# Row sums of one adjacency on ScalarE, x loads on GpSimd's queue, and the transposed adjacency stored in quarters

## The chip, the cores and the metric

The kernel runs on one core of a Trainium2 chip. The metric is device time of one execution in microseconds; the time before is the median of three runs. Each engine (TensorE or PE, VectorE or DVE, ScalarE or ACT, GpSimd or POOL, SyncE or SP) takes its instructions in order. Transfers are issued from the queue of an engine, here those of SP, ACT and POOL.

## The reference

Sixteen graphs of N = 1,024 nodes with C = 128 features, each with a dense 0/1 adjacency of 1,024 x 1,024. Layer 0 is a gated graph network of four steps behind a layer norm, layer 1 four graph convolutions with a batch norm over all nodes of all graphs; both add their result to x.

```python
def _gru_cell(m, h, w_ih, w_hh, b_ih, b_hh):
    xr, xz, xn = jnp.split(m @ w_ih.T + b_ih, 3, axis=-1)
    hr, hz, hn = jnp.split(h @ w_hh.T + b_hh, 3, axis=-1)
    r = jax.nn.sigmoid(xr + hr)
    z = jax.nn.sigmoid(xz + hz)
    n = jnp.tanh(xn + r * hn)
    return (1.0 - z) * n + z * h

# layer 0
h = jnp.maximum(_layernorm(x), 0.0)
for i in range(4):
    hw = jnp.einsum('bnc,cd->bnd', h, weight[i])
    m = jnp.einsum('bjn,bjd->bnd', adj, hw)       # adj transposed
    h = _gru_cell(m, h, w_ih[i], w_hh[i], b_ih[i], b_hh[i])
x = x + h * nodemask
# layer 1
h = jnp.maximum(_layernorm(x), 0.0)
for i in range(4):
    h = relu(jnp.einsum('bnm,bmc->bnc', adj, h @ W[i]) + b[i])
    mu, var = mean and variance of h over (batch, node)
    h = gamma[i] * (h - mu) * rsqrt(var + eps) + beta[i]
x = x + h
```

Layer 0 aggregates with the transposed adjacency, layer 1 with the adjacency itself; so one of the two has to be turned.

## The kernel before, in words

Features stay transposed, 128 channels on partitions and nodes in two halves of 512. The kernel has two stages.

**Stage 1 (layer 0)** runs two streams of batches, `sa` (even) and `sb` (odd), against each other. `half_step(one, two)` aggregates for one stream (`agg_step`, line 524: 32 matmuls of 128x512, the features split into a high and a low part) while the gates of the other are computed (line 1000: 24 matmuls). TensorE alternates between these two kinds; ScalarE copies the aggregate `m` (L961) and does the gates' functions (L1018, L1023, L1027), VectorE their products and the low part of the next split (L932, L1019 to L1044). There are 64 such half steps, eight to a pair of batches. The order on all five engines is written by hand here (`tc.manual_schedule`): what the Python code issues first stands first. Side work is put in through an agenda: `at(n, place, go)` names a half step and a place in it, and `due(place)` issues it there ("beside0", "beside1", "gap", "mid" and others are places in `half_step`).

Side work of stage 1 that matters here:

- *Node features.* `next_load` loads the 512 KB of x of the batch after next (L539, 14 loads) on ACT's queue. `norm_sums` (L664, L665) takes their statistics on VectorE within the same or the next half step. `xmid_d` and `ymid_d` (L752, L755) keep what stage 2 needs, stored on POOL's queue.
- *Raw adjacency.* Rows arrive in tiles `stage` on SP's queue and are cast to `row` on GpSimd (L577); `glance` (L586) takes a sum over each on ScalarE.
- *State exchange.* `cross_h` goes out and eight `n_h` come back on SP's queue (L591, L598); the split of the next step needs `n_h`.
- *The transposed adjacency for stage 2.* `transposes` is a generator that one call of `feed.some(n)` moves on by n rows. For a row it casts to bf16 on GpSimd (L615, tile `half`, two buffers) and issues a DMA transpose on SP's queue (L616) into `adjT`, a tile for one batch, of which there is one buffer. After eight rows the whole tile of 2 MB is stored to `adjT_d` from POOL's queue (L629). `Feed` keeps a flag `full` at the eighth row; then nothing more is fed until `mids` has issued the store in that or a later half step, and `next_step` clears the flag. `mids` first issues a small copy `pace` on GpSimd (L1101) that waits for the new state. Rows are fed in three places of a half step, with `counts` of (2, 1, 1), and more in two of a cycle's half steps.

**Stage 2 (layer 1)** loops over 4 layers and 16 batches. `load_adjT` reads a batch's packed adjacency on SP's queue, and casts on VectorE and ScalarE make `wide` from it (L1326, L1328). In layer 0 each batch also has its features split (`first_split`, L1383 to L1386, a ScalarE cast and a VectorE subtraction) and its weights applied to the aggregate (`first_weights`, the copies `cm` at L1395 and the matmuls `pw` at L1396). For the later layers, the batch norm is folded into the weights. The first batch after each batch norm (`raw_split`, `raw_weights`) has to add a term with the sum of every adjacency row; that sum, the same on every partition, lies in `degree` (L1413), which uses the memory of `w_mT` once stage 1 is over. `row_sums` makes it after the aggregation of stage 2's first batch: 16 matmuls of 128x512 with a matrix of ones (L1422) and two copies on ScalarE (L1426).

At the change of stages the order on VectorE and ScalarE is settled by a scheduler; in the last gate steps of stage 1 the order of TensorE, GpSimd and SP is still by hand.

Of the kernel before, what the change touches and what calls it, by code (L numbers as in the profile page):

```python
# [8 lines left out]
F32 = mybir.dt.float32  # L9
F32R = mybir.dt.float32r  # L10
BF16 = mybir.dt.bfloat16
# [5 lines left out]
P = 128  # L17
HALF = 512
# [323 lines left out]
def exact_path(  # L342
# [39 lines left out]
    def tmp(name):  # L382
        return ps_t.tile([P, HALF], F32, tag="tmp", name=name)

    adjT_d = [dram.tile([NB, P, N], BF16, tag=f"adjT{b}", name=f"adjT_d{b}") for b in range(B)]
    xmid_d = [dram.tile([N, C], F32, tag=f"xmid{b}", name=f"xmid_d{b}") for b in range(B)]
    ymid_d = [dram.tile([P, N], F32, tag=f"ymid{b}", name=f"ymid_d{b}") for b in range(B)]
# [10 lines left out]
    def turned_tile(name):  # L398
        return keep.tile([P, NB, N], BF16, tag="adjT", name=name, bufs=1)
# [8 lines left out]
    nc.vector.memset(eps_t, EPS)  # L408
    ones = const.tile([P, 1], F32, tag="ones", name="ones")
    nc.vector.memset(ones, 1.0)  # L410
    low = const.tile([P, (B + 2) * NB], F32, tag="low", name="low")
    nc.vector.memset(low, 0.0)

# [119 lines left out]
    with ExitStack() as st:  # L533
# [3 lines left out]
        def load_x(b, eng):  # L537
            xt = flat(f"x{b}")
            eng.dma_start(xt, x[b].rearrange("(k p) c -> p k c", p=P))  # L539
            return xt  # L540
# [39 lines left out]
        def glance(b, stage, js):  # L580

            junk = work.tile([P, N], BF16, tag="junk", name=f"junk{b}_{js[0]}", bufs=1)
            for j in js:
                lows = stage[j % 4].bitcast(U16).rearrange("p (n t) -> p n t", t=2)[:, :, 0]
                k = b * NB + j
                nc.scalar.activation(junk, lows, AF.Copy, accum_out=low[:, k : k + 1])  # L586

        def exchange_out(t, name, d=None):
            if d is None:
                d = rawd.tile([P, HALF], F32, tag="cross", name=f"cross_{name}", bufs=8)  # L590
            nc.sync.dma_start(d, t)  # L591
            return d
# [19 lines left out]
        def transpose_rows(b, row, j, adjT):  # L612

            t = work.tile([P, N], BF16, tag="half1", name=f"half{b}_{j}", bufs=2)
            nc.gpsimd.tensor_copy(t, row.bitcast(F32))  # L615
            return lambda: nc.sync.dma_start_transpose(adjT[:, :, j * P : (j + 1) * P], t)  # L616

        def transposes(batches):

            for b, rows in batches:  # L620
                adjT = turned_tile(f"adjT{b}")
                ahead = transpose_rows(b, rows[0], 0, adjT)
                for j in range(NB):
                    go = ahead
                    if j + 1 < NB:
                        ahead = transpose_rows(b, rows[j + 1], j + 1, adjT)
                    go()
                    yield j
                nc.gpsimd.dma_start(adjT_d[b].rearrange("k p n -> p k n"), adjT)  # L629
                yield NB  # L630

        class Feed:


            jobs, full, stored = iter(()), False, False

            def some(self, n):
                for _ in range(n):
                    if not self.full:
                        self.full = next(self.jobs, None) == NB - 1  # L640

            def store(self):
                if self.full and not self.stored:
                    self.stored = next(self.jobs) == NB

            def next_step(self):
                if self.stored:
                    self.full = self.stored = False

        feed, agenda = Feed(), {}  # L650

# [118 lines left out]
        class Stream:  # L770
# [35 lines left out]
                norm_blocks(self.xt, self.y, self.norm, ks)  # L806

            def next_load(self):
                self.next_x = load_x(self.b + 2, nc.scalar)

            def next_sums(self):
                self.next_norm = norm_stats(self.next_x, f"in{self.b + 2}")
# [256 lines left out]
        def at(n, place, go):  # L1069
            agenda.setdefault((n, place), []).append(go)  # L1070
# [4 lines left out]

        def first_step(one, two, gated, halfway):

            feed.next_step()
            if one is sa:
                feed.jobs = transposes([(s.b, s.rows) for s in (sa, sb)])  # L1080
            one.split_step()
            feed.some(2)
            two.gate_step(0)
            two.half_away(0)
            if feed.full or (clock[0], "mid") in agenda:
                mids(two)
            feed.some(1)
            two.gate_step(1)
            two.half_away(1)
            gated()  # L1090
            one.agg_step(0)
            halfway()
            feed.some(NB if one is sa else 1)
            one.agg_step(1)
            two.finish()
            clock[0] += 1

        def mids(two):

            pace = small.tile([P, 1], F32, tag="pace", name=f"pace{clock[0]}")  # L1100
            nc.gpsimd.tensor_copy(pace, two.new[:, :1])  # L1101
            feed.store()
            due("mid")

        def half_step(one, two, gated=None, halfway=None):

            feed.next_step()
            counts = (2, 1, 1)
            if one is sb and one.i == 0:
                feed.jobs = transposes([(s.b, s.rows) for s in (sa, sb)])  # L1110
                counts = (0, 0, 0)
            elif two is sb and two.i == 0:
                counts = (2, 2, 1)
            elif two is sa and two.i == 1 and two.across:
                counts = (3, 1, 1)
            due("ins")
            due("start")
            if one.i > 0:
                one.halves_back()
            else:  # L1120
                one.hw = hw_tiles(one.b, f"ghw{one.b}_0")
            two.fetch()
            feed.some(counts[0])
            two.products(0)
            two.reset_gate(0)
            due("beside0")
            due("looks")
            two.fetch_more()
            two.candidate(0)
            two.less(0)  # L1130
            two.update_gate(0)
            two.scaled()
            one.high(0)
            one.low(0)
            two.mixed(0)
            two.half_away(0)
            two.first_four()
            if feed.full or (clock[0], "mid") in agenda:
                mids(two)
            feed.some(counts[1])  # L1140
            two.products(1)
            two.reset_gate(1)
            one.high(1)
            due("beside1")
            two.first_glances()
            one.low(1)
            two.candidate(1)
            two.less(1)
            two.update_gate(1)
            two.last_four()  # L1150
            two.scaled()
            two.mixed(1)
            two.half_away(1)
            due("outs")
            if gated:
                gated()
            due("gap")
            due("end")
            one.agg_step(0)
            if halfway:  # L1160
                halfway()
            feed.some(counts[2])
            one.agg_step(1)
            two.finish()
            clock[0] += 1
# [4 lines left out]
        with tc.manual_schedule(engines=every):  # L1170
# [111 lines left out]
            def ahead(i):  # L1282
                join_layer(i)
                if i + 1 < L:
                    turn_hh(i + 1)

            sa.plan(0)
            sb.plan(1)
            first_step(sa, sb, looks, lambda: ahead(1))
            first_step(sb, sa, lambda: turn_ih(prep, w_g, 2), lambda: ahead(2))  # L1290
            written[0] = False
# [89 lines left out]
    def first_split(b):  # L1381
        yt = flat(f"y{b}").rearrange("p k c -> p (k c)")
        nc.gpsimd.dma_start(yt, ymid_d[b])  # L1383
        hw = hw_tiles(b, f"chw{b}_0")
        nc.scalar.copy(hw[0], yt)
        nc.vector.tensor_sub(hw[1], yt, hw[0].bitcast(F32))  # L1386
        return hw

# [17 lines left out]
    def raw_weights(i, pm, aff, stats):  # L1406
# [6 lines left out]
            nc.vector.scalar_tensor_tensor(mt[:, cols], degree[:, cols], aff[1], mt[:, cols], ALU.mult, ALU.add)  # L1413
            nc.tensor.matmul(pc[hf], w_c[:, i, :], mt[:, cols], start=True, stop=True)
        conv_done(0, i, pc, stats)

    def row_sums(rows):

        pd = [tmp(f"pt_deg{hf}") for hf in range(NH)]
        for j in range(NB):  # L1420
            for hf in range(NH):
                nc.tensor.matmul(  # L1422
                    pd[hf], ones_r, rows[j][:, hf * HALF : (hf + 1) * HALF], start=(j == 0), stop=(j == NB - 1)
                )
        for hf in range(NH):
            nc.scalar.copy(degree[:, hf * HALF : (hf + 1) * HALF], pd[hf])  # L1426

    xo = []

# [29 lines left out]
            for n0, n in pieces(k):  # L1459
                nc.gpsimd.dma_start(xo_piece(k, n0, n), by_node(xmid_d[k], n0, n))  # L1460

    ones_r = work.tile([P, P], F32R, tag="ones_r", name="ones_r", bufs=1)
    nc.vector.tensor_copy(ones_r, ones.to_broadcast([P, P]))
    degree = w_mT.rearrange("p l c -> p (l c)")[:, :N]

    stats = small.tile([P, B * NH, 6], F32, tag="bn_st", name="stats0")
# [1 line left out]
    for b in range(B):  # L1468
        rows = load_adjT(b, 0)
        hw_next = first_split(b + 1) if b + 1 < B else None  # L1470
        pm = banks(b, 0)
        aggregate(pm, hw, rows, 0)
        if waiting:
            last = first_weights(*waiting, stats)
            if b == 1:
                with tc.issue_after(last.ins):
                    sb.rest()
        if b == B - 1:
            hw_next = raw_split(1)
        aggregate(pm, hw, rows, 1)  # L1480
        if b == 0:
            row_sums(rows)
        hw, waiting = hw_next, (b, pm)


# [112 lines left out]
```

## Time and profile before

| | us |
|---|---|
| three runs | 1769.65, 1770.71, 1772.32 |
| median | 1770.71 |
| the profiled execution, time | 1769.17 |
| the profiled execution, span of the core | 1767.4 |
| TensorE busy | 1752.3 |
| VectorE busy | 1289.3 |
| ScalarE busy | 1112.0 |
| GpSimd busy | 362.9 |

The profile is one execution on the chip. The span goes from its first to its last recorded event; 1.8 us of the profiled execution's own time lie around it. A group names its line, engine, operation, and output and input tiles. Busy time of TensorE is close to time that its matmuls follow one another; their durations overlap, so that spacing is read from starts. In a list of waits, three numbers are the total in us, how often, and the longest. A timeline row has start and duration in us, and in brackets the idle time before it with what ended it.

### The profile page before, as it was taken

Reading aid. Unit: us, or ns where it says so; the run is one execution under the profiler, and the core shown is the slowest. Engines: PE = TensorE matmul, PEld = TensorE weight load, DVE = VectorE, ACT = ScalarE, POOL = GpSimd, SP = SyncE. Lnnn points to the kernel's source line nnn. Section 1 sums busy time; section 2 is a strip of 40 time slices with the busy share of each in tenths; the row PEclk is TensorE's granted clock in tenths of the full one; section 3 lists DMA queues with packets and bytes.
Section 4 is the critical chain, followed back from the end, with each engine's and each line's share of the span. In section 5 each row is a group of like instructions: output and inputs, shape, how many; then the busy total and the mean of one; then the engine's idle time right before and its main releaser. Section 6 shows DMA issues by size and latency. Waiting matters only on the chain. (4 is left out here: it accounts for less than half of the span.)

```text
span 1767.4 us, 22310 instructions
## 1 busy us (share of the span) xinstructions
PE 1752.3 (99%) x6734; PEld 1192.7 (67%) x6734; DVE 1289.3 (73%) x2310; ACT 1112.0 (63%) x1713; POOL 362.9 (21%) x401
## 2 busy tenths in 40 slices
PE   9999999999999999999999999999999999999997
PEld 5565656565656565656565656577778888888886
DVE  7677877877877887877887786766666666666665
ACT  5356556557556556655655664487677767767765
POOL 4214213322332331321422323110100000000011
PEclk9999999999999999999999999999999999999999
DMA  7458568577686676776866857887866665757667
GB/s 261 138 169 280 166 180 301 158 223 248 196 214 221 221 212 216 238 197 200 270 185 178 305 137 228 287 290 289 292 220 215 234 243 210 256 202 258 230 220 270
DMA packets 376160, 400.14 MB, mean 226 GB/s; under 512 B 158188, under 2 KB 254224, under 8 KB 376032
## 3 DMA queue, kind: packets, MB, share of 16 engines
q1 hardware_dynamic: 342736, 323.59, 58.0%
q0 software_dynamic: 18208, 67.46, 10.2%
q10 hardware_dynamic: 15088, 7.60, 1.5%
q8 instruction: 54, 0.88, 0.2%
q14 instruction: 74, 0.61, 0.1%
HBM read 267.47 MB, written 97.52 MB: 207 GB/s over the span
## 5 line engine op out<-in xcount | busy, mean ns | idle before, releaser
L524 PE MATMUL pm<-row,ghw 128*128 128x512 f32 x2048 | 503.9, 403 | 0.5 <-POOL row L563 0.3
L524 PEld LDWEIGHTS pm<-row,ghw 128*128 128x128 f32 x2048 | 383.6, 188 | 107.1 <-issue 25.6
L524 PE MATMUL pc_m<-wide,chw 128*128 128x512 f32 x1024 | 245.2, 395 | 0.0
L615 POOL CAST half<-row 128x1024 bf16<-128x1024 f32 x128 | 143.7, 1133 | 402.3 <-DMA adjT<-half 387.4
L524 PEld LDWEIGHTS pc_m<-wide,chw 128*128 128x128 f32 x1024 | 190.4, 188 | 41.9 <-issue 3.8
L961 ACT COPY m<-pm 128x512 f32<-128x512 f32 x128 | 68.7, 588 | 195.4 <-PE pm L524 195.4
L1023 ACT ACTIVATE r<-r,vecs 128x512 f32<-128x512 f32 x128 | 92.2, 721 | 152.8 <-DVE r L1020 148.8
L524 PE MATMUL pc_g_r<-wide,chw 128*128 128x512 f32 x464 | 186.9, 403 | 0.3 <-ACT chw L501 0.3
L1019 DVE SCALAR_TENSOR_TENSOR r<-g_hn,vecs,r 128x512 f32<-128x512 f32 x128 | 93.3, 729 | 128.5 <-ACT r L1018 76.3
L524 PE MATMUL pc_g_z<-wide,chw 128*128 128x512 f32 x464 | 181.0, 390 | 0.0
L577 POOL CAST row<-stage 128x1024 fp32r<-128x1024 f32 x112 | 128.1, 1151 | 207.4 <-DMA stage<-in_adj_dram 198.7
L1328 DVE CAST wide<-block 128x1024 fp32r<-128x1024 bf16 x160 | 110.0, 692 | 73.7 <-PE pc_m L524 36.6
L1328 DVE CAST wide<-packed 128x1024 fp32r<-128x1024 bf16 x160 | 110.1, 691 | 71.8 <-PE pc_g_z L524 53.7
L1326 ACT CAST wide<-packed 128x1024 fp32r<-128x1024 bf16 x96 | 100.7, 1049 | 58.5 <-PE pc_m L524 30.3
L1326 ACT CAST wide<-block 128x1024 fp32r<-128x1024 bf16 x96 | 100.6, 1049 | 53.8 <-PE pc_g_z L524 27.7
L1000 PE MATMUL g_r<-m,w_mT 128*128 128x512 f32 x256 | 130.8, 592 | 0.3 <-ACT m L961 0.3
L1000 PE MATMUL g_z<-m,w_mT 128*128 128x512 f32 x256 | 130.7, 592 | 0.0
L1000 PE MATMUL g_xn<-m,w_mT 128*128 128x512 f32 x256 | 130.7, 592 | 0.0
L1018 ACT ACTIVATE r<-g_r,brz 128x512 f32<-128x512 f32 x128 | 87.9, 686 | 53.9 <-PE g_r L1000 53.4
L1376 DVE BATCH_NORM_STATS2 stats<-feat 128x6 f32<-128x512 f32 x128 | 84.1, 686 | 47.0 <-ACT feat L1375 45.9
L1036 DVE TENSOR_TENSOR h<-h,r 128x512 f32<-128x512 f32 x96 | 78.9, 821 | 54.1 <-ACT r L1023 53.9
L1040 DVE TENSOR_TENSOR h<-h,z 128x512 f32<-128x512 f32 x128 | 105.3, 822 | 14.1 <-ACT z L1027 2.1
(185 smaller groups left out, 2810.8 us busy)
## 6 DMA issues: line engine op xcount, KB each, us to landing
block<-adjT_d SPq DMA_DIRECT2D x256, 256.0 KB, 4.7
packed<-adjT_d SPq DMA_DIRECT2D x256, 256.0 KB, 5.7
stage<-in_adj_dram SPq DMA_DIRECT2D x120, 512.0 KB, 5.4
adjT_d<-adjT POOLq DMA_DIRECT2D x16, 2048.0 KB, 7.8
cross_h<-t_h SPq DMA_DIRECT2D x92, 256.0 KB, 2.1
n_h<-cross_h SPq DMA_DIRECT2D x368, 64.0 KB, 2.0
xmid_d<-x POOLq DMA_DIRECT2D x16, 512.0 KB, 6.7
y<-ymid_d POOLq DMA_DIRECT2D x16, 512.0 KB, 5.2
```

Of the source, the lines that this page charges most:

```text
L524: nc.tensor.matmul(pm[hf], hw[s][:, j * P : (j + 1) * P], rows[j][:, hf * HALF : (hf + 1) * HALF], start=(j == 0 and s == 0), stop=(j == N ...
L577: nc.gpsimd.tensor_copy(t, stage[j % 4])
L615: nc.gpsimd.tensor_copy(t, row.bitcast(F32))
L1000: nc.tensor.matmul(po, wT[:, i, g * C : (g + 1) * C], rhs, start=start, stop=stop)
L1018: nc.scalar.activation(r, pr, AF.Sigmoid, bias=brz[:, 3 * i : 3 * i + 1])
L1019: nc.vector.scalar_tensor_tensor(r, phn, b_hn(i), r, ALU.add, ALU.mult)
L1023: nc.scalar.activation(self.r, self.r, AF.Tanh, bias=b_in(self.i))
L1036: nc.vector.tensor_sub(ho, hin, self.r)
L1040: nc.vector.tensor_mul(ho, ho, self.z)
L1326: nc.scalar.copy(r, t)
L1328: nc.vector.tensor_copy(r, t)
L1376: nc.vector.bn_stats(stats[:, b * NH + hf, :], dst)
```

## The change

It has four parts.

1. The row sums are no longer made by matmuls in stage 2. In stage 1, eight ScalarE instructions (`row_sums` inside `exact_path`'s stage 1, with `accum_out`) sum the rows of batch 0 as they lie in memory: one at each of four places, one in half step 5 and three in half step 6, three in the gap of half step 7, and one at the start of half step 8. At half step 9 POOL's queue stores the 4 KB of sums; at the third batch of stage 2 it loads them back to all partitions, into `degree`. The matrix `ones_r`, the 16 matmuls and the two copies are gone.
2. `next_load` issues on POOL's queue instead of ACT's.
3. `transposes` handles both batches of a pair in one tile, without a stop between them. After every second row, two rows' columns of `adjT` are stored: four stores of 512 KB per batch. The flags of `Feed`, `store` and `next_step` are gone, `counts` is (2, 1, 1) throughout, and `mids` runs only where the agenda has something for "mid".
4. In `first_split` the ScalarE cast is put behind `sb.last_m`, the last copy of an aggregate in stage 1.

```diff
-            for b, rows in batches:
-                adjT = turned_tile(f"adjT{b}")
-                ahead = transpose_rows(b, rows[0], 0, adjT)
-                for j in range(NB):
-                    go = ahead
-                    if j + 1 < NB:
-                        ahead = transpose_rows(b, rows[j + 1], j + 1, adjT)
-                    go()
-                    yield j
-                nc.gpsimd.dma_start(adjT_d[b].rearrange("k p n -> p k n"), adjT)
-                yield NB
+            adjT = turned_tile(f"adjT{batches[0][0]}")
+            steps = [(b, rows, j) for b, rows in batches for j in range(NB)]
+            def cast(s):
+                b, rows, j = steps[s]
+                return transpose_rows(b, rows[j], j, adjT)
+            def store(b, q):
+                cols = slice(2 * q * P, 2 * (q + 1) * P)
+                nc.gpsimd.dma_start(adjT_d[b][:, :, cols].rearrange("k p n -> p k n"), adjT[:, :, cols])
+            ahead = cast(0)
+            for s, (b, rows, j) in enumerate(steps):
+                go = ahead
+                if s + 1 < len(steps):
+                    ahead = cast(s + 1)
+                if s > 1 and s % 2 == 0:
+                    store(steps[s - 1][0], steps[s - 1][2] // 2)
+                go()
+                yield
+            store(steps[-1][0], NB // 2 - 1)
+            yield
...
+        def row_sums(rows, js):
+            for j in js:
+                junk = work.tile([P, N], BF16, tag="junk", name=f"summed{j}", bufs=1)
+                nc.scalar.activation(junk, rows[j].bitcast(F32), AF.Copy, accum_out=by_row[:, j : j + 1])
...
-                self.next_x = load_x(self.b + 2, nc.scalar)
+                self.next_x = load_x(self.b + 2, nc.gpsimd)
...
-            feed.store()
             due("mid")
...
-            feed.next_step()
             counts = (2, 1, 1)
             if one is sb and one.i == 0:
                 feed.jobs = transposes([(s.b, s.rows) for s in (sa, sb)])
                 counts = (0, 0, 0)
-            elif two is sb and two.i == 0:
-                counts = (2, 2, 1)
-            elif two is sa and two.i == 1 and two.across:
-                counts = (3, 1, 1)
...
-            if feed.full or (clock[0], "mid") in agenda:
+            if (clock[0], "mid") in agenda:
                 mids(two)
...
+            for n, place, js in (
+                (5, "beside1", (0,)),
+                (6, "beside0", (1,)),
+                (6, "beside1", (2,)),
+                (6, "gap", (3,)),
+                (7, "gap", (4, 5, 6)),
+                (8, "start", (7,)),
+            ):
+                at(n, place, lambda js=js: row_sums(sa.rows, js))
+            at(9, "mid", lambda: nc.gpsimd.dma_start(degree_d.rearrange("(j p) -> p j", p=P), by_row))
...
-        nc.scalar.copy(hw[0], yt)
+        with tc.issue_after(sb.last_m.ins):
+            nc.scalar.copy(hw[0], yt)
...
-        if b == 0:
-            row_sums(rows)
+        if b == 2:
+            nc.gpsimd.dma_start(degree, degree_d.partition_broadcast(P))
```

More of the change, by code (lines that the diff above doesn't have):

```diff
@@ L383, in tmp @@
         return ps_t.tile([P, HALF], F32, tag="tmp", name=name)
+    degree_d = dram.tile([N], F32, tag="degree", name="degree_d")
     adjT_d = [dram.tile([NB, P, N], BF16, tag=f"adjT{b}", name=f"adjT_d{b}") for b in range(B)]
@@ L410, in exact_path @@
     nc.vector.memset(ones, 1.0)
+    by_row = const.tile([P, NB], F32, tag="by_row", name="by_row")
     low = const.tile([P, (B + 2) * NB], F32, tag="low", name="low")
@@ L618, in transposes @@
         def transposes(batches):
-            for b, rows in batches:
-                adjT = turned_tile(f"adjT{b}")
-                ahead = transpose_rows(b, rows[0], 0, adjT)
-                for j in range(NB):
-                    go = ahead
-                    if j + 1 < NB:
-                        ahead = transpose_rows(b, rows[j + 1], j + 1, adjT)
-                    go()
-                    yield j
-                nc.gpsimd.dma_start(adjT_d[b].rearrange("k p n -> p k n"), adjT)
-                yield NB
+            adjT = turned_tile(f"adjT{batches[0][0]}")
[17 more added lines that the diff above has]
+            yield
         class Feed:
-            jobs, full, stored = iter(()), False, False
+            jobs = iter(())
             def some(self, n):
                 for _ in range(n):
[L639 to L648, printed above, removed]
+                    next(self.jobs, None)
         feed, agenda = Feed(), {}
@@ L1081, in first_step @@
             one.split_step()
-            feed.some(2)
+            feed.some(2 if one is sa else 0)
             two.gate_step(0)
             two.half_away(0)
-            if feed.full or (clock[0], "mid") in agenda:
+            if (clock[0], "mid") in agenda:
                 mids(two)
-            feed.some(1)
+            feed.some(1 if one is sa else 0)
             two.gate_step(1)
@@ L1092, in first_step @@
             halfway()
-            feed.some(NB if one is sa else 1)
+            feed.some(NB - 3 if one is sa else 0)
             one.agg_step(1)
@@ L1101, in mids @@
             nc.gpsimd.tensor_copy(pace, two.new[:, :1])
-            feed.store()
             due("mid")
         def half_step(one, two, gated=None, halfway=None):
-            feed.next_step()
             counts = (2, 1, 1)
@@ L1137, in half_step @@
             two.first_four()
-            if feed.full or (clock[0], "mid") in agenda:
+            if (clock[0], "mid") in agenda:
                 mids(two)
@@ L1415, in raw_weights @@
         conv_done(0, i, pc, stats)
[L1417 to L1426, printed above, removed]
     xo = []
@@ L1460, in fetch_x @@
                 nc.gpsimd.dma_start(xo_piece(k, n0, n), by_node(xmid_d[k], n0, n))
-    ones_r = work.tile([P, P], F32R, tag="ones_r", name="ones_r", bufs=1)
-    nc.vector.tensor_copy(ones_r, ones.to_broadcast([P, P]))
     degree = w_mT.rearrange("p l c -> p (l c)")[:, :N]
```

## The prediction

> **What bounds the kernel now.** I read the page's first two sections, then the waits, then the timelines of the three places that the change touches.
>
> ```profile
> PE 1752.3 (99%) x6734; PEld 1192.7 (67%) x6734; DVE 1289.3 (73%) x2310; ACT 1112.0 (63%) x1713; POOL 362.9 (21%) x401
> PEclk9999999999999999999999999999999999999999
> POOL half L615 <- DMA adjT<-half: 387.4, 66, 18.3
> ACT m L961 <- PE pm L524: 195.4, 62, 5.8
> POOL adjT_d L629 <- DMA adjT<-half: 16.9, 7, 5.1
> ACT ghw L925 <- DMA n_h<-cross_h: 12.4, 13, 2.4
> ```
>
> TensorE is busy 99% of 1767.4 us at full clock. So the time is the number of matmuls times their spacing, plus what TensorE waits, and that is some 15 us in all, most of it at the two ends and in the batchnorm turns, which the change leaves alone. An edit gains only by taking matmuls from TensorE or by ending one of its few waits; it loses by making a new one. Of the waits shown, the 387 us of GpSimd for the transposes cost nothing now (TensorE never waits for them), but they say that GpSimd's queue stands still a good fifth of the time: whatever is put into it in order stands still too. 195 us over 62 waits is ScalarE arriving about 3.15 us early at each half step's `m`: that is its spare time there.
>
> The one stretch in which matmuls go away:
>
> ```profile
> 1158.37 0.39 PE L524 MATMUL pc_g_r<-wide,chw 128*128 128x512 f32 x1
> 1158.77 3.89 PE L1422 MATMUL pt_deg<-wide,ones_r 128*128 128x512 f32 x16
> 1162.50 0.39 PE L524 MATMUL pc_g_z<-wide,chw 128*128 128x512 f32 x1
> ```
>
> Columns: start, duration, work. Starts, not durations, give the cost, since matmuls overlap: L524's are 0.227 us apart (1162.50, 1162.72, 1162.95 ...). From 1158.37 to 1162.50 are 4.13 us; without the 16 they would be 0.23.
>
> The one wait in the middle of the kernel that the change addresses (TensorE, then ScalarE):
>
> ```profile
> 1119.09 1.12 PE L1000 MATMUL g_r<-m,w_mT 128*128 128x512 f32 x2 [0.30 <-ACT m L961]
> 1117.51 1.05 ACT L1385 CAST chw<-y 128x1024 fp32r<-128x1024 f32 x1 [5.77 <-PE pm L524]
> 1118.46 1.07 ACT L961 COPY m<-pm 128x512 f32<-128x512 f32 x2
> ```
>
> The cast for stage 2's first batch got in ahead of the last `m`; the gates wait for `m`.
>
> **The change part by part.**
> *Row sums off TensorE (gain).* 4.13 - 0.23 = 3.90 us, if what follows can come 3.9 us sooner. What is added: 8 ScalarE sums over 128x1024 with an accumulator. The row of that shape is L586, 1.05 us + 0.19 to read the accumulator, spaced about 1.17: 9.4 us on ScalarE in half steps 5 to 8. One at a time they are shorter than the 1.65 us that y blocks (L680) take in the same slots of other half steps without a TensorE wait. The three in half step 7's gap (3.5 us) fit between the end of the square root at 128.85 and `m` at 133.16 with 0.8 to spare. The one at the start of half step 8 delays r by 1.15 us; the low half of the weights is then ready at about 141.95 by the chain, needed 143.4. Cost 0; the cover is ScalarE's spare time, 3.15 us in each of four half steps against 9.4 us of sums, so only a badly placed sum can show: up to 1 us. The two `pt_deg` copies (1.06 us of ScalarE) go. The sums are written once by GpSimd's queue (1,024 runs, as many as xmid_d's: 0.90 to issue, 6.7 to land; in runs of 4 bytes it may be slower, but nothing needs it for 900 us) and read back as 512 KB spread over partitions at the third batch of stage 2; the raw batch's `degree` is wanted only after the layer's statistics, 120 us later. Cost 0, between 0 and 1 us: a gain is excluded, since TensorE waits for nothing there.
>
> *The weight cast put behind the last `m` (gain).* 0.46 + 0.10 us of gaps around 1118.2 to 1119.1 go: 0.56. The cast itself is wanted only at the first aggregation of stage 2, 20 us later. What is late next: nothing until the last gates.
>
> *x from GpSimd's queue (14 loads).* ScalarE is rid of 14 issues of 0.41 us in half steps in which it has 3 us to spare: 0. On GpSimd's queue:
>
> ```profile
> 506.53 0.42 ACTq L539 DMA_DIRECT2D x<-in_x_dram  x1
> 512.37 1.04 POOL L615 CAST half<-row 128x1024 bf16<-128x1024 f32 x1 [11.23 <-DMA adjT<-half]
> 518.43 0.25 DVE L664 BATCH_NORM_STATS2 st_in<-x 128x6 f32<-128x128 f32 x1
> 522.65 0.75 DVE L1019 SCALAR_TENSOR_TENSOR r<-g_hn,vecs,r 128x512 f32<-128x512 f32 x1 [1.00 <-PE g_hn L1000]
> x<-in_x_dram ACTq DMA_DIRECT2D x14, 512.0 KB, 4.6
> xmid_d<-x POOLq DMA_DIRECT2D x16, 512.0 KB, 6.7
> ```
>
> In the changed order x stands right behind that cast, which waits for transposes. So it is issued at about 513.4 + 0.9 of GpSimd's time (xmid_d's row) instead of 506.5, and lands 4.6 to 6.7 us after 513.4: 518.0 to 520.1. VectorE's sums, due at 518.43, start up to 1.7 us late; VectorE idles 1.0 behind them, and its low-part subtraction (L932, ends 527.17) has 2.5 us before the aggregation that begins at 529.71. Late by 1.7, covered by 3.5: cost 0; the other loads, one half step on, have 2.65 us of idle VectorE behind the sums and are 0 to 2 late. Here the Trainium skill speaks against the change: "SBUF — State Buffer", section "SBUF: two separate sides", says that transfers issued by GpSimd have their descriptors written by its cores, which are locked out while VectorE runs a two-port operation, and to issue from ScalarE or SyncE instead. The rows: 512 KB took 4.6 us from ScalarE, 6.7 and 5.2 (y) from GpSimd. By the rule the landing is at the upper end or past it, 2 us late in seven cycles; by the row it is inside the 3.5 us. I take the row: 0. Both ends kept: 0 to +14 (rival 2).
>
> *Four stores of 512 KB in place of one of 2 MB, both batches in one tile.* Per batch GpSimd issues 4 x 0.90 = 3.6 us in place of 0.90 (all rows of GpSimd with about 1,000 runs: adjT_d 0.90, xmid_d 0.90); 16 batches: 43 us more on an engine that is 21% busy and stands waiting for transposes anyhow. The transposes themselves stay 128, at four per half step; a transpose now waits for a quarter's store instead of a whole tile's. A store waits for the landing of its two transposes (2.8 us), and the casts, the x load and the pace copies queue behind it; the next cast needs that transpose's buffer anyway. SyncE: the order of transposes against cross_h and n_h changes; one of 1.25 us now stands between the last cross_h and its eight n_h. In the half steps in question n_h now lands late because the 2 MB store fills the engines (a ghw wait of up to 2.4 us, above, and about 0.55 us left before TensorE would see it). Cutting the store in four takes that away and the transpose puts 1.3 back: even. The skill speaks against small pieces: "DMA: Bandwidth & Descriptors", section "Anatomy of one DMA — SWDGE (gpsimd) path", prices a transfer at 2.0 us + bytes/436e3, so an estimate of 6.8 us for 2 MB (the row: 7.8) and 4 x 3.2 = 12.8 for four. The rows for 512 KB from GpSimd are 3.5 to 6.7. Either way the pieces go out over two half steps (35 us), so the sum by rule and by row is the same 0 for TensorE as long as nobody waits for a store; the last one at the change of stages does matter: reads of the first packed adjacency can begin about 13 us sooner (1107.5 instead of 1120.95). Half of a small TensorE gap of 0.44 us near 797.6 may go: 0.2.
>
> *The change of stages.* The order moves: ScalarE's table loads and square root (1.28 + 0.30 + 1.28) now stand before the last tanh, and packed casts before the last `m` copies. By a count through the chain the last state is ready for its transposes at about 1153.0, TensorE comes to them (27 matmuls of the first batch done instead of 14) at 1153.1: 0 to 1 us. With deg gone, TensorE wants the second batch's copies `cm` 3.9 us sooner, at 1169.4; ScalarE has them at 1169.1: 0 to 1 us. I take 0.3 each.
>
> **Sum**: -3.90 - 0.56 - 0.2 + 0.3 + 0.3 = -4.06, say -4.1: 1769.17 - 4.1 = 1765.1 for the profiled run (span 1767.4 and 1.8 around it), which ran 1.5 below the median; on the median 1770.71 - 4.1 = 1766.6.
>
> **Rivals.**
> 1. *The row sums were cover.* Around 1160 nobody but TensorE had time:
>
> ```profile
> 1160.00:1180.00 20.00, 20.00 (x82) 15.07 (x81) 13.96 (x22) 18.49 (x30) 2.19 (x3) 1.00 0.94 341
> ```
>
> (TensorE, weight loads, VectorE, ScalarE, GpSimd busy, clock, DMA share, GB/s.) ScalarE 18.49 of 20 and DMA 0.94: take 3.9 us of matmuls out, and casts, reads of 2 MB per batch or `cm` become the bound for a batch or two. For it: those numbers. Against: only this stretch is so full; from 1180 ScalarE is 13.56 of 20, and 1.06 us of `pt_deg` copies go as well, while packed reads begin earlier. It would take back 1 to 3.5 us: 1767.5 to 1770.
> 2. *x behind GpSimd's waits makes it slower.* The place: half steps 5, 13, ... (seven). It decides when x lands later than 518.43 + 3.5 = 521.9, or 8.5 us after the cast that frees it. Casts on GpSimd come 3.9 us apart when transposes hold them (514.03, 517.96, 521.85); one more such wait in front puts x at 517.3 to issue and 521.9 to 524.0 landed: up to 2.1 us each, 7 times, 15 us, if the n_h chain with its 0.55 us of room slips too. 1766.6 + 4 (two of the seven, or all by little) to + 15: 1771 to 1782. For it: 387 us of waits in that queue, and stores added to it. Against: by the order x stands behind no further wait, and the rows leave 1.8 us even at the late end.
> 3. *The row sums don't reach their slots:* a sum in half step 7 or 8 holds up `m` once, 1 us: 1767.6, within 0.2%.
>
> **How the numbers follow.** My forecast 0.51 (1764.3 to 1767.2), rival 1 0.22, rival 2 0.23, rival 3 0.04. About 0.2%, 3.5 us, is what this measurement can tell from no change; the forecast passes it by 0.6 only. Faster 0.51 (the forecast), same 0.26 (rivals 1 and 3), slower 0.23 (rival 2). Alone the forecast has 1764.3 to 1767.2, its lower end with the two 0.3s not paid and the 1.5 us by which one run differs from another; the range goes on up to 1777, to hold over half of rival 2.
>
> **What would show it.** No `pt_deg`; TensorE busy about 1748.5; no gap before g_r near 1118. x's landing in half steps 5, 13, ... before 521.9 on the old clock, so half steps still 17.57 us each, and ghw's waits for n_h no larger than 12.4 us in all. Wrong if TensorE shows repeated gaps every eighth half step (rival 2), or gaps of over 1 us between 1150 and 1180 (rival 1).

## The result, and the profile after

The changed kernel takes 1813.53 us (median of five, 1809.91 to 1823.36) against 1770.71 (five runs as well; the table above has their lowest, middle and highest): 1.0253 times as long, 95% interval 1.022 to 1.0287. The forecast was 1766.6. The profiled execution is the longest of the five, 1823.36 us with a span of 1821.6; the shape of its loss is what is read here, and medians carry the sizes.

The first section of its page, the row of TensorE's clock, and its DMA issues with the median time to landing:

```profile
PE 1766.5 (97%) x6718; PEld 1192.6 (65%) x6718; DVE 1284.9 (71%) x2309; ACT 1121.0 (62%) x1729; POOL 414.2 (23%) x457
PEclk9999999999999999999999999999999999999999
cross_h<-t_h SPq DMA_DIRECT2D x92, 256.0 KB, 2.8
n_h<-cross_h SPq DMA_DIRECT2D x368, 64.0 KB, 2.6
x<-in_x_dram POOLq DMA_DIRECT2D x14, 512.0 KB, 9.2
adjT<-half SPq DMA_TRANSPOSE x128, 5.6
```

Two lines of the kernel before, to set beside these and beside the waits below:

```profile
adjT<-half SPq DMA_TRANSPOSE x128, 2.8
DVE st_in L664 <- DMA x<-in_x_dram: 3.2, 1, 3.2
```

Sixteen matmuls are gone (6734 to 6718), as they should be, and yet TensorE is busy for longer. The four kinds of transfer shown land later than before: x 9.2 us after its issue instead of 4.6, a transpose 5.6 instead of 2.8, cross_h 2.8 instead of 2.1, n_h 2.6 instead of 2.0. The waits say where that ends (total us, times, longest):

```profile
PE g_hn L1009 <- DVE r L1028: 27.4, 11, 5.8
PE pm L526 <- ACT ghw L934: 6.1, 3, 4.4
DVE st_in L673 <- DMA x<-in_x_dram: 80.0, 16, 9.0
```

In the kernel before, VectorE waited once for x, 3.2 us at the start. Now it waits 16 times. One of them, on GpSimd, VectorE and TensorE, in order of time (rows in between left out):

```profile
405.78 1.04 POOL L623 CAST half<-row 128x1024 bf16<-128x1024 f32 x1 [6.06 <-DMA adjT<-half]
411.72 1.04 POOL L623 CAST half<-row 128x1024 bf16<-128x1024 f32 x1 [4.91 <-DMA adjT<-half]
420.74 1.20 POOL L623 CAST half<-row 128x1024 bf16<-128x1024 f32 x1 [7.15 <-DMA adjT<-half]
421.88 0.89 POOL L541 DMA_DIRECT2D x<-in_x_dram  x1
428.27 1.02 PE L1009 MATMUL g_r<-m,w_mT 128*128 128x512 f32 x2
431.08 0.29 DVE L673 BATCH_NORM_STATS2 st_in<-x 128x6 f32<-128x128 f32 x1 [9.01 <-DMA x<-in_x_dram]
434.26 0.73 DVE L1028 SCALAR_TENSOR_TENSOR r<-g_hn,vecs,r 128x512 f32<-128x512 f32 x1
435.05 2.08 PE L1009 MATMUL g_hn<-h,w_hhT 128*128 128x512 f32 x2 [5.76 <-DVE r L1028]
436.91 1.91 PE L1009 MATMUL g_xn<-m,w_mT 128*128 128x512 f32 x2
```

GpSimd's cast waits for transposes, x is issued right behind it, and lands 9.2 us later. The sums of x stand in front of `r` in VectorE's order, so `r` waits with them. TensorE's next `g_hn` waits for `r`, 5.76 us. That is the prediction's second rival in kind, x too late behind GpSimd's casts, but not in its details: no further cast stands in front of x; the casts come 5.9 and 9.0 us apart instead of 3.9, the landing takes 9.2 us, and this is the later of a cycle's two loads, not the earlier one that the rival named. Behind it comes what no part of the prediction held: matmul starts of 853 ns instead of 429. The windows show the clock (columns as before: busy time per engine, clock, DMA share, GB/s):

```profile
421.00:429.00 8.00, 8.00 (x23) 3.86 (x21) 1.00 (x4) 4.58 (x8) 4.32 (x6) 1.00 0.78 125
429.00:435.00 6.00, 0.29 (x1) 0.00 (x0) 3.63 (x17) 0.00 (x0) 0.00 (x0) 0.74 1.17 232
435.00:440.00 5.00, 4.95 (x9) 2.17 (x9) 2.50 (x4) 2.37 (x4) 0.89 (x1) 0.63 1.07 186
440.00:460.00 20.00, 20.00 (x67) 12.41 (x66) 15.01 (x24) 16.72 (x32) 2.25 (x3) 1.00 0.59 201
```

The granted clock averages 0.74 over 6 us in the wait and 0.63 over the 5 us behind it: at half rate, that is 3.1 and 3.7 us. In this run the same follows every wait of TensorE from 2.84 us up (0.57 from 582 to 586 us, behind the one of 2.84), and none of 2.64 or less (1.00 from 1018 to 1026 us). From 110 us on, TensorE's waits in stage 1 make some 32 us, and it is busy for 16.9 us at half rate, which loses 8.5 more; most of what else the cycles lose, listed below, lies in gaps of under 0.3 us. In the kernel before, TensorE has no wait of over 0.3 us there and no stretch at half rate. The Trainium skill states this gate ("TensorE: Matmul & The Clock Gate", "Part 1: The HAM clock gate"): half rate after an idle window of about 3.4 us, full rate after as long a busy one. The two rates agree with the starts; the waits that set it off are in part shorter here, and their length alone does not decide (keep_32 below, after a wait of 1.89 us: 0.57 from 552 to 556 us). The row of tenths in the page hides it.

By cycle of eight half steps the kernel before takes 140.6 us each (one of 141.1). The changed one takes 147.3, 151.4, 149.8, 146.4, 145.9, 146.2 and 143.9, and has lost 7.9 us before the first of these. Stage 2 is shorter. So all the loss is in stage 1 and comes back in each cycle.

### The profile page after: what moved, and what is told of

Same layout as the page of the kernel before. It is cut to its first block, busy times and chain, and to the rows that moved or that the text cites. A ratio compares the mean times of both kernels' runs of the same rounds, so it can differ in the third digit from the quotient of the medians.

```text
span 1821.6 us, 22354 instructions
## 1 busy us (share of the span) xinstructions
PE 1766.5 (97%) x6718; PEld 1192.6 (65%) x6718; DVE 1284.9 (71%) x2309; ACT 1121.0 (62%) x1729; POOL 414.2 (23%) x457
## 5 line engine op out<-in xcount | busy, mean ns | idle before, releaser
L1009 PE MATMUL g_xn<-m,w_mT 128*128 128x512 f32 x256 | 134.7, 609 | 0.0
L1009 PE MATMUL g_hn<-h,w_hhT 128*128 128x512 f32 x192 | 102.7, 617 | 27.4 <-DVE r L1028 27.4
L1049 DVE TENSOR_TENSOR h<-h,z 128x512 f32<-128x512 f32 x128 | 113.7, 888 | 14.5 <-ACT z L1036 1.7
```

The lines of the kernel that those rows point to most:

```text
L1009: nc.tensor.matmul(po, wT[:, i, g * C : (g + 1) * C], rhs, start=start, stop=stop)
L1049: nc.vector.tensor_mul(ho, ho, self.z)
```

## The experiments

All times are medians, beside the kernel before on the same chip (1770.0 to 1770.5 us), most with a ratio.

**First round: undo one part, or both.**

```diff
-                self.next_x = load_x(self.b + 2, nc.gpsimd)    # x_act
+                self.next_x = load_x(self.b + 2, nc.scalar)
...
-                    at(n + 5, "beside0", self.next_load)       # load_5start
+                    at(n + 5, "start", self.next_load)
```

x_act: 

> The changed kernel with one edit: x is loaded on ACT's queue again. Theory 1 (x comes late because it stands in GpSimd's queue): the 80 us that VectorE waited for x go, the gaps before g_hn go, 1767 to 1773 us, what is left being n_h and m. Theory 2 (the four stores run beside the transposes and stretch every transfer, whoever issues it): x is still slow, though issued some 7 us sooner; transposes stay at 6 to 9 us, n_h stays late, 1780 to 1800 us.

Measured: 1782.47 us, ratio 1.0068 (1.0046 to 1.0091).

old_store (`transposes`, `Feed` and `counts` of the kernel before, x on GpSimd's queue): 

> The changed kernel with the transposes, the store and the counts as before; x stays on GpSimd's queue. Theory 1 (queue): x stays behind the casts that wait for transposes, 1795 to 1815 us. Theory 2 (stores beside transposes): transposes are back at 2.8 us, x lands 5 to 7 us after its issue, VectorE waits for it by under 3 us at a time, 1766 to 1774 us.

Measured: 1781.12 us, 1.0057 (1.0044 to 1.007).

sums_only (both undone): 

> The changed kernel with both undone: only the row sums on ScalarE and the cast behind the last m are left. Both theories: 1766.6 us, 4.1 below the kernel before, by the prediction's own sum; 1768 to 1770 if the change of stages takes the gain back.

Measured: 1775.99 us, 1.0035 (1.0022 to 1.0048).

load_5start: 

> The changed kernel with x still on GpSimd's queue, issued at the start of its half step instead of beside the first gates, so that one or two casts (which wait for transposes) stand behind it instead of ahead. Theory 1: x is issued 4 to 8 us sooner and lands in time, 1768 to 1778 us. Theory 2: it lands 9 us after its issue still, VectorE's waits fall from 5 to 9 us to under 4, 1775 to 1795 us.

Measured: 1779.91 us, 1.0055 (1.0043 to 1.0067); VectorE's waits for x fell from 80.0 us to 3.8, and x landed 6.7 us after its issue.

Each of the three runs that undo or move one part takes 31 to 34 us off, so neither theory has the loss to itself, and neither was met: x_act lies above the range of theory 1, but its transposes (4.5 us) are faster than theory 2 had them; old_store lies between the two ranges; load_5start lies in the range of theory 2, but x lands sooner than that theory had it. Both theories are wrong for sums_only. With x and the stores as they were, that kernel is 6 us slower than the kernel before, 9 above the sum of the prediction, and TensorE's new waits (`g_z` for ScalarE's z, 4.4 us in four places against 0.6 in one) are in later cycles, where not one instruction differs from the kernel before. In that run, too, packets took longer, throughout stage 1. What had changed for them was where tiles lie. The row sums are kept in a new tile of 32 bytes a partition, allocated ahead of the two pools that hold x, the rows, adjT and the states. In the kernel before, the tiles of these pools begin at multiples of 256 bytes; in the changed one, all begin 32 bytes past one.

**Second round: the beginning of the tiles alone.**

```diff
-    by_row = const.tile([P, NB], F32, tag="by_row", name="by_row")
+    by_row = const.tile([P, 8 * NB], F32, tag="by_row", name="by_row")[:, :NB]
```

after_256: 

> The changed kernel with one edit: the tile of the eight row sums is 256 bytes a partition instead of 32, of which 32 are used. In the changed kernel every large tile that lies behind it (x, rows, adjT, half, the states) begins at 32 bytes past a multiple of 256; with the edit they begin at multiples of 256 as in the kernel before. Theory 3 (it is the shift by 32 bytes that slows the transfers): packets are back at 27 ns for 512 bytes and 18 for 256, x lands within 7 us, 1766 to 1775 us. Theories 1 and 2 (queue and stores alone): 1805 to 1820 us as without the edit.

Measured: 1767.34 us, 0.9985 (0.9978 to 0.9991).

sums_256: 

> Only the row sums on ScalarE and the cast behind the last m, with the 256-byte tile. Theory 3: the 4.1 us of the prediction's sum come out, 1765 to 1767.5 us. Without theory 3: 1776 as with the 32-byte tile.

Measured: 1766.75 us, 0.9979 (0.9972 to 0.9985).

The kernel before gets an unused tile at the same place:

```diff
+    gap32 = const.tile([P, NB], F32, tag="gap32", name="gap32")
+    nc.vector.memset(gap32, 0.0)
     low = const.tile([P, (B + 2) * NB], F32, tag="low", name="low")
```

before_32: 

> The kernel before with nothing but an unused tile of 32 bytes a partition at the place of the row sums' tile (and its memset at the start). Theory 3: 1775 to 1781 us, 5 to 11 slower, with 512-byte packets at 33 ns in the mean instead of 28.7. Without it: 1770 us.

Measured: 1778.26 us, 1.0043 (1.003 to 1.0057).

before_64 (`[P, 2 * NB]`): 

> The same with 64 bytes: the tiles begin 64 bytes past a multiple of 256. If what counts is a multiple of 64, 1770 us as before; if it is a multiple of 256 (or of 512), 1775 to 1781 us.

Measured: 1777.52 us, 1.0043 (1.0029 to 1.0056).

This settles it: one number in a shape, no instruction moved, and the changed kernel goes from 1813.53 to 1767.34. The reverse holds too: an unused tile makes the kernel before 8 us slower. The DRAM tiles lie as before in that kernel, so it is not they. Its engines are not slower at their work either. Three lines of before_32:

```profile
PE 1754.7 (99%) x6734; PEld 1192.9 (67%) x6734; DVE 1281.5 (72%) x2311; ACT 1112.2 (63%) x1713; POOL 366.6 (21%) x401
PE g_z L1002 <- ACT z L1029: 5.4, 6, 2.4
adjT<-half SPq DMA_TRANSPOSE x128, 3.5
```

VectorE and ScalarE are busy 1281.5 and 1112.2 us against 1289.3 and 1112.0 before. What grows is the transfers (a transpose 3.5 us instead of 2.8), ScalarE's waits for n_h (29.7 us instead of 12.4), and behind them TensorE's for z. From the packet records of stage 1 (until 1100 us), ns of one (512 bytes: SP's queue alone; the last column of the last two rows has x's loads in it as well, so it compares these two with each other):

| kernel | tiles begin at | 256 bytes, mean | 512 bytes, mean (75%, 90%) | 4,096 from GpSimd's queue, mean |
|---|---|---|---|---|
| before | 0 | 20.6 | 28.7 (27, 27) | 172.8 |
| before_32 | 32 | 23.2 | 33.1 (34, 48) | 189.2 |
| before_64 | 64 | 23.3 | 32.3 (32, 46) | 189.3 |
| before_128 | 128 | 23.0 | 31.4 (27, 44) | 188.8 |
| after_256 | 0 | 22.6 | 30.4 (27, 36) | 212.2 |
| after | 32 | 28.3 | 35.8 (40, 51) | 262.6 |

The median of the first two stays at 18 and 27 in all: a part of the packets takes longer.

Waits and landings of the changed kernel with its tiles in place, to set beside those of the changed kernel above:

```profile
DVE st_in L673 <- DMA x<-in_x_dram: 20.6, 11, 4.2
x<-in_x_dram POOLq DMA_DIRECT2D x14, 512.0 KB, 6.7
adjT<-half SPq DMA_TRANSPOSE x128, 4.4
ACT ghw L934 <- DMA n_h<-cross_h: 5.7, 4, 3.0
```

VectorE still waits for x, 11 times, but never for over 4.2 us, and no wait of TensorE for `r` of any size is left.

**Third round: the parts again with tiles in place, and single tiles out of place.** x_act_256 and old_store_256 are the first round's kernels with the 256-byte tile. For x_32, the 32-byte tile lies in the pool right ahead of x and a pad of 224 bytes behind it; for adjT_32, the same around adjT:

```diff
-    by_row = const.tile([P, NB], F32, tag="by_row", name="by_row")
...
+            by_row = keep.tile([P, NB], F32, tag="by_row", name="by_row", bufs=1)
             x0 = flat("x0")
+            pad = keep.tile([P, 56], F32, tag="pad", name="pad", bufs=1)
+            nc.vector.memset(pad, 0.0)
```

x_act_256: 

> The changed kernel with the 256-byte tile and x on ACT's queue again: row sums, the cast behind the last m, and the four stores. With the tiles in place the prediction priced the move of x at nothing: 1767.3 us as with x on GpSimd's queue, between 1766 and 1769. A theory that x on ACT's queue holds ScalarE up (its load waits there for the store of xmid_d) gives 1769 to 1772.

Measured: 1770.09 us, 0.9997 (0.9989 to 1.0006).

old_store_256: 

> The changed kernel with the 256-byte tile and the transposes, store and counts as before; x stays on GpSimd's queue. The prediction priced the stores at nothing: 1766.5 to 1767.5 us. If the pieces cost something of their own: 1766 or less.

Measured: 1766.65 us, 0.9979 (0.997 to 0.9988).

x_32: 

> The changed kernel with all large tiles at multiples of 256 bytes but those of x, which begin 32 past one. If every tile suffers in its own transfers alone: x's loads (14 of 512 KB and the stores of x and ymid) are a small part of the traffic, 1768 to 1775 us. If it is x's late landing that makes the 46 us: 1785 us and more.

Measured: 1769.98 us, 0.9998 (0.999 to 1.0007).

adjT_32: 

> The changed kernel with all large tiles at multiples of 256 bytes but adjT, into which the transposes write and from which the stores read: it begins 32 past one. If it is the transposes and stores that stretch everything else: 1785 to 1810 us, transposes at 5 us. If it is spread over all tiles: 1770 to 1780 us.

Measured: 1769.47 us, 0.9995 (0.9986 to 1.0003).

**Fourth round: halves of memory, and 128 bytes.** In keep_32 the tiles of one pool are out of place (x, adjT, most rows, the states in exchange), in work_32 those of the other (the bf16 rows that transposes read, y, states of the streams, the other rows). For keep_32 the pad of 224 bytes comes first in the second pool; for work_32 the 32-byte tile does:

```diff
         work = st.enter_context(tc.tile_pool(name="work", bufs=2))
+        by_row = work.tile([P, NB], F32, tag="by_row", name="by_row", bufs=1)
```

keep_32: 

> The changed kernel with the tiles of the keep pool (x, adjT, most rows, the exchanged states) 32 bytes past a multiple of 256, and those of the work pool at multiples. If the exchange of states and x land late enough to pass what VectorE has to spare: 1785 to 1810 us. If the transposes' own source rows (work pool) are needed for it: 1772 to 1778 us.

Measured: 1787.79 us (1780.21 to 1790.5), 1.0105 (1.0089 to 1.012).

work_32: 

> The other way round: only the work pool's tiles (half rows that the transposes read, y, h, some rows) are shifted. If the transposes' reads are what stretches: 1780 to 1800 us, transposes at 5 us and over. If it is the keep pool: 1768 to 1772 us. If it is only both together, both runs stay under 1780 us, and what decides is the sum of small delays against a fixed room.

Measured: 1778.58 us, 1.0049 (1.0035 to 1.0062).

before_128 (`[P, 4 * NB]`): 

> The kernel before with an unused tile of 128 bytes a partition: tiles begin at multiples of 128 that are not multiples of 256. If 256 is what counts: 1775 to 1779 us, as with 32 and 64. If 128 is enough: 1770 us.

Measured: 1777.44 us, 1.0038 (1.0024 to 1.0052). 32, 64 and 128 cost the same; with 256 (sums_256, after_256) the cost is gone.

The tiles' cost against x's landing, over after_256's 1767.34 us. Costs are of medians; landings and waits are of one profiled run each (keep_32's was its fastest, 1780.21):

| out of place | over after_256, us | x lands after | VectorE waited for x, longest |
|---|---|---|---|
| none | 0 | 6.7 | 20.6, 4.2 |
| x | 2.6 | 8.2 | 32.0, 3.8 |
| adjT | 2.1 | 7.2 | 29.9, 6.4 |
| work pool | 11.2 | 7.7 | 29.3, 4.4 |
| keep pool | 20.4 | 8.1 | 46.5, 6.2 |
| both pools (the changed kernel) | 46.2 | 9.2 | 80.0, 9.0 |

11.2 and 20.4 make 31.6, not 46.2, and x with adjT only 4.7 of the keep pool's 20.4: no single tile that was tried is the culprit. The last column does not order the costs by itself, for a wait of VectorE is paid only where it passes the room behind it. keep_32 fell in its first range; work_32 lies 1.4 us under the range for the work pool, and adjT_32 0.5 us under the range for a cost spread over all tiles. In keep_32's profile TensorE waits for `r` in three half steps (3.7 us), in the changed kernel in eleven (27.4); work_32's loss lies for the most part in the first two cycles, with 0.7 us in each later one.

Those 0.7 us, and 0.5 in keep_32's quiet cycles, are no waits and no transfers: a half step there takes 17.66 and 17.63 us instead of 17.57, because the same matmuls of each aggregation start 231 to 236 ns apart instead of 227, the last eight among them. The moving operands of these eight lie in the work pool and their weights in the keep pool, so in these two runs one of the two is 32 bytes past a multiple of 256 and the other is not. In the changed kernel, where both pools are shifted alike, the quiet half steps take 17.57 as before. Over stage 1 this is 5.5 us of work_32's cost and 3.8 of keep_32's (estimates from the starts until 1200 us), which the changed kernel does not pay; the transfers' part of 31.6 is nearer to 22. Why the offset matters there stays open.

Which of the other tiles (the exchanged states, rows, the bf16 rows) gives how much stays open. The same growth is seen in the parts:

| over the kernel before, us | tiles in place | 32 bytes past |
|---|---|---|
| row sums and the cast only | -3.5 | +6.0 |
| with x on GpSimd's queue | -3.9 | +11.1 |
| with the four stores | -0.4 | +12.5 |
| with both (the change) | -3.0 | +43 |

Shifted, x costs 5 us alone, the stores 6.5, and both 37. In place, the two together cost 0.6. With the tiles in place, no more is gained than the row sums and the cast bring: sums_256 (1766.75) and old_store_256 (1766.65) are the fastest kernels here and cannot be told apart.

## Why the prediction was wrong

*The failing step is one that was not in the sum.* The row sums were priced by their instructions (removed, added, waited for), and the tile that they need at nothing, without being named. It is a term like the others: 32 bytes a partition cost some 8 to 10 us by themselves (before_32, +8.0; sums_only against sums_256, +9.2), and 46.2 with the other parts. The Trainium skill bears on it in "DMA: Bandwidth & Descriptors", section "How a descriptor splits into AXI transactions": a read starts at a 256-byte boundary, and a descriptor that starts elsewhere fetches bytes that it does not use. For 512 bytes from 32 past a boundary that is an estimate of 17 beats for 16, in three transactions for two, so 6% by the one count and half as much again by the other; the mean of 512-byte packets rose by 15% in before_32. That the beginning of a tile slows packets is shown; that this splitting is why is the page's account, and not shown here. Its transactions are three for 32, 64 and 128 alike, as the costs are alike; its beats (17, 18 and 20) are not, and it speaks of reads, while x's loads write the tiles.

*x on GpSimd's queue.* With the tiles in place, issue was placed right: 513.4 forecast, 512.96 in a kernel that is 2.3 us later there. Landing was put at 4.6 to 6.7 us: 6.7 there, but 9.2 as the kernel stood, with the issue late as well behind slower transposes. The point from which it decides held roughly: TensorE waits for `r` only where x lands 8.4 us or more after its issue, though not at every such place. What was mis-sized is the price past that point, 2.1 us a half step in the rival: TensorE waited up to 5.8 us, and longest in the later half step of a pair, which the prediction had set aside as covered; it waited for `r`, where the prediction had counted its room to the low part of the split; and the slower clock came on top. So even the rival's 1771 to 1782 fell short of 1813.5. The rule that was weighed against the row there (VectorE locking out GpSimd's descriptors) is not needed for the loss: with the tiles in place the same queue lands x in 6.7 us (5.1 with the stores as before, old_store_256), and TensorE waits for none of it.

*The four stores.* The prediction laid n_h's waits to the one store of 2 MB and took its quarters as even. With the tiles in place, ScalarE's waits for n_h are 12.5 us with that store and x on ACT's queue (sums_256), 4.3 with that store and x on GpSimd's (old_store_256), 20.6 with quarters and x on ACT's (x_act_256), and 5.7 with both parts of the change. So the move of x lowers them and the quarters raise them, the other way round from the reading in the prediction. Transposes are slower with the quarters: 3.7 us instead of 2.9 with x on ACT's queue, 4.4 in the whole change, and that was left out. With x on ACT's queue the stores' part costs 3.3 us over sums_256 (x_act_256), all of it before the first of the cycles listed above: TensorE waits 1.7 us there for z and 1.4 for `w_both`, behind a wait of ScalarE for n_h of 2.8. By what way the stores' part brings that wait stays open.

*What was right,* read in the changed kernel with its tiles in place. `pt_deg` is gone, and from the first matmul of stage 2 to the first matmul of its second layer's weights it takes 140.15 us against 143.73: 3.58 less, where 3.90 less 0.33 was the sum for it. The 0.33 is the delay of the last state's transposes, priced at 0.3 (the first line; six matmuls from 1153.66 on, 0.227 apart, put it due at 1155.02):

```profile
1155.35 0.63 PE L744 MATMUL pt_x<-ident,h 128*128 128x128 f32 x4 [0.17 <-DVE h L1053]
1119.68 1.02 PE L1009 MATMUL g_r<-h,w_hhT 128*128 128x512 f32 x2
1120.54 1.02 PE L1009 MATMUL g_r<-m,w_mT 128*128 128x512 f32 x2
```

The second and third line are the gates that waited 0.56 us for `m`: 0.86 apart now, no wait. The second batch's `cm` kept nobody waiting, so rival 1 (the row sums as cover) did not come; stage 2 keeps its gain. The gap near 797 is gone (all later cycles are 140.6). Against it stand 2.3 us more before the first of those cycles. They come with the stores' part: 3.5 in x_act_256, 0.1 in sums_256, 0.0 in old_store_256. At the last matmuls of this one profiled run 2.3 us are gained; the medians give 3.0 for it, and 3.5 for row sums and cast alone, of the 4.1 forecast. So the sum for the row sums and the cast was right by its mechanism, and it is covered up, not refuted, in the changed kernel.

## What to carry to other kernels

Where a change adds a buffer, however small, look at where every buffer behind it comes to lie: round it up to 256 bytes a partition, as was done here (putting it last was not tried). When a part that touches nothing late slows every late cycle, compare packet times before instruction times. And when two transfers share a fixed room, price them together: shifted, x and the stores cost 5 and 6.5 us alone here and 37 together, since only what passes the room is paid, and a wait long enough is paid again in slower matmuls.

## What the runs showed of the hardware

- SBUF tiles 32, 64 or 128 bytes past a multiple of 256 made the kernel before 7.1 to 8.0 us slower (0.4%) with nothing else changed, though the median packet of 256 and of 512 bytes took as long as before; the tail grew (512 bytes at the 90th percentile: 27 to 48 ns with 32 bytes).
- After TensorE had waited 5.76 us, the next matmuls started 853 ns apart instead of 429, for 3.6 us. In the profiled run of the changed kernel half rate followed waits from 2.84 us up, in keep_32 one of 1.89, and in the former it lost 8.5 us (16.9 us at half rate, an estimate from the windows) beside some 32 us of waits.
- With one of two pools 32 bytes past a multiple of 256 and the other on one (work_32, keep_32), some of an aggregation's matmuls started 231 to 236 ns apart instead of 227; with both pools on multiples (the kernel before) or both 32 past (the changed kernel) they did not.
